# Softmax denominators on VectorE: one reciprocal for each sum, turned and spread, in place of 32 equal ones

## The chip, the cores and the metric

The kernel runs on one core of a Trainium2 chip. The metric is the device time of one execution in microseconds (us): before the change 3507.78 us, the median of three runs (3505.2 to 3508.09).

## The reference

One transformer block with adaptive layer norm, 8 sequences of 1024 tokens of width 512, in float32. Cut to what matters:

```python
mod = silu(condition) @ Wada + bada            # six shifts, gains and gates for each sequence
sh_a, sc_a, gt_a, sh_m, sc_m, gt_m = split(mod, 6)
xm = layernorm(x, g1, be1) * (1 + sc_a) + sh_a
q, k, v = heads(xm @ Wqkv)                     # 16 heads of 32 columns
scores = where(causal, q @ k.T * 32 ** -0.5, -inf)
attn = softmax(scores)                         # exp(s - max) / sum of exp(s - max)
x = x + gt_a * (concat(attn @ v) @ Wproj + bproj)
xm = layernorm(x, g2, be2) * (1 + sc_m) + sh_m
x = x + gt_m * (gelu(xm @ W1 + b1) @ W2 + b2)
```

## The kernel before, in words

The work is cut into 16 blocks of 512 tokens (n, two per sequence). The 16 heads of a block are handled in 4 groups (g) of 4 heads, so there are 64 groups. The keys and queries of a group lie with head and channel on the 128 partitions: head j on partitions 32j to 32j+31.

Attention of a group runs in units. `scores` (L1538) multiplies queries by keys into PSUM (L1595), VectorE adds the causal mask (L1607) and takes row maxima (L1610). The maxima are split into three bfloat16 parts (L1629 to L1632) and turned into rows by TensorE (L1648). `weights_T` (L1663) subtracts the maxima (L1674) and multiplies keys by queries (L1686), ScalarE takes the exponential (L1698), and GpSimd cuts the diagonal (L1703). `weigh` (L1715) multiplies the weights by the values (L1726). `add_weights` (L1801) adds the weights of later keys to those of the first, nearly always on GpSimd (L1816).

`finish` (L1736) ends a group. A matmul with a matrix of ones (L1747) sums the weights over the keys. Its columns are 32 ones for each head, so the sum of head j for token t stands on all 32 partitions of head j: 32 equal rows. ScalarE copies the sums to `rec` (L1756) and the weighted values to `top` (L1759). VectorE inverts `rec` in place in four pieces of 128 columns (`invert`, L1765), and `top` is multiplied by it: by GpSimd in most groups (L1790), by VectorE in three cases. `rec` and `top` have one buffer each, so L1756 of the next group waits for this multiplication. The groups differ in how that is queued:

- the last group of all (`groups[-1]`): inversions and multiplications alternate, piece by piece, at once (L1769 to L1773)
- the last group of block 0 (`first_end`): four inversions and a multiplication on VectorE (L1779), at once
- the other 62: three inversions as jobs, and a fourth job (`quotient`) with the last inversion and the multiplication

The rest of the block is linear work: the projections for k, q, v and the first layer of the MLP by a seven-product scheme (`strassen`), the second layer (`down`) likewise, the output projection (`project_out`), all through `matmul` (L217). Layer norm needs statistics (L619, L620), normalisation (L655, L660), and a turn to channel-first form, for most blocks by VectorE in squares of 32 (L700) and two DMAs (L709, L714). The results of a matmul leave PSUM through `copy_out` (L194, L197) and `combine_out` (L204, L208).

The order of everything is fixed when the program is built. A planner keeps a clock for each engine in `now`; `note` adds a cost in ns to an engine's clock, `due` says when operands are ready. From these clocks `sooner` (L152) picks VectorE or ScalarE, and `either` (L159) picks VectorE (L167) or GpSimd (L170) for an elementwise operation. Jobs wait in one list; `run_jobs` (L558) issues the first job whenever VectorE's clock isn't ahead of TensorE's and its operand is due. `step_aside` (L1457) and `work` (L1423) choose which matmuls come next. So a cost given to `note` decides nothing on the chip itself, but it moves instructions in all queues.

Of the kernel before, what the change touches and what calls it, by code (L numbers as in the profile page):

```python
# [9 lines left out]
F32 = mybir.dt.float32  # L10
# [12 lines left out]
def kernel(  # L23
# [33 lines left out]
    nc = tc.nc  # L57
    B, T, D = x.shape
    HD = W1.shape[1]
    P = 128  # L60
    hd = D // H
    scale = float(hd) ** -0.5
    TB = 512
    NTT = TB // P
    NHALF = T // TB
    NC = D // P
# [15 lines left out]
    small = ctx.enter_context(tc.tile_pool(name="small", bufs=2))  # L82
# [22 lines left out]
    def due(reads=(), writes=()):  # L105
        t = 0.0
        for k in reads:
            t = max(t, written.get(k, 0.0))
        for k in writes:
            t = max(t, left.get(k, 0.0))  # L110
        return t

    def note(engine, ns, reads=(), writes=(), port=False):
        start = max(now[engine], due(reads, writes))
        if port:
            start = max([start] + [b for a, b in pool_spans if a <= start < b])
        end = start + ns
        now[engine] = end
        if engine == "POOL":
            pool_spans.append((start, end))  # L120
            del pool_spans[:-16]
        for k in reads:
            left[k] = max(left.get(k, 0.0), end + SYNC)
        for k in writes:
            written[k] = end + SYNC
        return end
# [9 lines left out]
    def note_pe(ns, form, reads=(), writes=()):  # L136
        now["PE"] = max(now["PE"], due(reads, writes))
        if shape[0] != form:
            shape[0] = form
            now["PE"] += SWITCH  # L140
        note("PE", ns, reads)
        spent[0] += ns
        for k in writes:
            written[k] = now["PE"] + PIPE

    def note_act(ns, func, reads=(), writes=()):
        if func is not None and table[0] != func:
            table[0] = func
            ns += TABLE
        note("ACT", ns, reads, writes)  # L150
# [31 lines left out]
    def lin_bank():  # L182
        i = min(
            (i for i in range(3) if not live[i]),
            key=lambda i: left.get(("l", i), 0.0),
        )
        live[i] = True
        return i
# [54 lines left out]
    def mlp_steps(n):  # L243
        return [("u", n, i) for i in range(NQ)] + [("d", n, part) for part in range(4)]
# [9 lines left out]
    for w in range(1, NB):  # L254
        n = w - 1
        m = mlp_steps(n)
# [29 lines left out]
    n = NB - 1  # L286
# [111 lines left out]
    Q = P // NTT  # L398
# [81 lines left out]
    def spread(o):  # L480
        return cols[:, o : o + NC].unsqueeze(2).to_broadcast([P, NC, B])

    def norm_columns(name, shift_at, gain_at, o_g, o_b):

        gain = const.tile([P, NC, B], F32, tag=f"gain{name}", name=f"gain{name}")
        shift = const.tile([P, NC, B], F32, tag=f"shift{name}", name=f"shift{name}")
        one_plus = small.tile([P, NC, B], F32, tag="onep", name=f"onep{name}")
        nc.vector.tensor_scalar(one_plus, modT[:, ts(gain_at, NC), :], 1.0, None, ALU.add)
        nc.vector.tensor_tensor(gain, one_plus, spread(o_g), ALU.mult)
        nc.vector.tensor_tensor(shift, one_plus, spread(o_b), ALU.mult)  # L490
        nc.vector.tensor_tensor(shift, shift, modT[:, ts(shift_at, NC), :], ALU.add)
        return gain, shift
# [60 lines left out]
    def add_job(job, reads, first=False):  # L553

        at = sum(1 for other in jobs if other[2]) if first else len(jobs)
        jobs.insert(at, (job, reads, first))

    def run_jobs(everything=False):  # L558
        while jobs and (
            everything or (now["DVE"] <= now["PE"] and due(jobs[0][1]) <= now["PE"])  # L560
        ):
            jobs.pop(0)[0]()
# [774 lines left out]
    def perform(step):  # L1337
        kind = step[0]
        if kind == "mod":
            yield from modulation(step[1])  # L1340
        elif kind == "norm_columns_a":
            columns_of["a"] = norm_columns("a", 0, 1, O_G1, O_BE1)
        elif kind == "gates":
            yield from gates(step[1])
        elif kind == "columns_m":
            columns_of["m"] = norm_columns("m", 3, 4, O_G2, O_BE2)
        elif kind == "load_xa":
            x_pre[step[1]] = load_x(step[1])
# [108 lines left out]
    def step_aside(reads, writes):  # L1457


        while threads():  # L1460
            if linear_wait() == NEVER:
                hurry()
            own, other = wait_of((reads, writes)), linear_wait()
            if done_linear[0] < stream["due"]:
                if other > own + 100:
                    break
            elif own <= max(other, 50):
                break
            work()
        while BANK in writes and bank_at() == NEVER:  # L1470
            work()
        run_jobs()
        run_act_jobs()
        run_pool_jobs()
        run_preparation()
# [260 lines left out]
    def finish(n, g):  # L1736

        run_jobs(True)
        acc, slot = totals.pop((n, g))
        more = unadded if (n, g) == first_end else []  # L1740
        step_aside([("acc", n, g), *(("p", slot) for *_, slot in more)], [BANK])
        bank = lin_bank()
        terms = [(0, TB, acc, slot)] + [(c0, w, pT, slot) for parts, pT, slot in more for _, c0, w, _ in parts]
        for i, (c0, w, term, held) in enumerate(terms):
            for j in range(HPG):
                r = slice(j * hd, (j + 1) * hd)
                nc.tensor.matmul(  # L1747
                    banks[bank][r, TB - w :], ones, term[:, j, c0 : c0 + w],
                    start=i == 0, stop=i == len(terms) - 1, skip_group_check=True,
                )  # L1750
            note_pe(2 * COLUMN * w, "columns", [("acc", n, g), ("p", held)], [("l", bank)])
        free_p.extend([slot, *(held for *_, held in more)])
        top = tmp.tile([P, TB], F32, tag="top", name=f"top_{n}_{g}", bufs=1)
        rec = tmp.tile([P, TB], F32, tag="rec", name=f"rec_{n}_{g}", bufs=1)
        kr = "rec"
        nc.scalar.copy(rec, banks[bank])  # L1756
        note_act(585, None, [("l", bank)], [kr])
        live[bank] = False
        nc.scalar.copy(top, outs.pop((n, g)))  # L1759
        note_act(585, None, ["po"], ["top"])  # L1760
        part = TB // 4

        def invert(i):
            some = rec[:, i * part : (i + 1) * part]
            nc.vector.reciprocal(some, some)  # L1765
            note("DVE", 920, [kr], [kr])

        if (n, g) == groups[-1]:
            for i in range(NTT):  # L1769
                invert(i)  # L1770
                some = slice(i * part, (i + 1) * part)
                nc.vector.tensor_tensor(qTs[n][:, g, some], top[:, some], rec[:, some], ALU.mult)
                note("DVE", 200, [kr, "top"], [("att", n, i)])  # L1773
            return

        if (n, g) == first_end:
            for i in range(NTT):
                invert(i)
            nc.vector.tensor_tensor(qTs[n][:, g, :], top, rec, ALU.mult)  # L1779
            note("DVE", 700, [kr, "top"], [("att", n)], port=True)  # L1780
            written["attended", n] = 0.0
            return

        def quotient():
            invert(3)
            if n == NB - 1 and g == NC - 2:
                nc.vector.tensor_tensor(qTs[n][:, g, :], top, rec, ALU.mult)
                note("DVE", 700, [kr, "top"], [("att", n)], port=True)
            else:
                nc.gpsimd.tensor_tensor(qTs[n][:, g, :], top, rec, ALU.mult)  # L1790
                note("POOL", 1285, [kr, "top"], [("att", n)])
            if g == NC - 1:
                written["attended", n] = 0.0

        for i in range(3):
            add_job(lambda i=i: invert(i), [kr], g == NC - 1)
        add_job(quotient, [kr], g == NC - 1)

    shared = {}
# [194 lines left out]
```

## Time and profile before

| | |
|---|---|
| median of three runs | 3507.78 us |
| the profiled execution | 3510.74 us |
| its span, first to last instruction | 3509.0 us |
| TensorE clock granted | 0.998 |
| TensorE (PE) busy | 3454.3 us, 98% |
| VectorE (DVE) busy | 2198.9 us, 63% |
| GpSimd (POOL) busy | 2084.2 us, 59% |
| ScalarE (ACT) busy | 1212.4 us, 35% |

The profile is one execution on the chip. Times are in microseconds unless marked ns; L1765 is line 1765 of the kernel. PE is TensorE's matmul, PEld its weight load, SP the engine that issues most DMAs. A row of a group has the line, engine, operation, destination and sources, shapes and count, then the busy time in us and the mean ns of one, then the idle time of the engine just before and what ended most of it. A row "A <- B: x, y, z" of the waits says that A sat idle for x us in total, y times, longest z, until B was done. A timeline row has start and length in us, engine, line and operation, and in brackets the idle time before it. Matmuls overlap and their ends are modelled, so TensorE's busy time is not all streaming. The "chain" is the work that ended last, followed back from the last instruction.

### The profile page before, as it was taken

How to read it: one execution, taken by the hardware profiler on the slowest of the kernel's cores; microseconds unless marked ns; L12 is line 12 of the kernel's file. 1: busy time of each engine (PE TensorE's matmuls, PEld its weight loads, DVE VectorE, ACT ScalarE, POOL GpSimd, SP SyncE). 2: the span in 40 equal slices, each digit the busy share in tenths (PEclk: the TensorE clock that was granted, in tenths of full speed). 3: DMA queues.
4: the chain of work that ended last, by engine and by line, in shares of the span. 5: the costliest groups of instructions: out<-in, count | busy, mean ns of one | idle time of the engine just before them, and what ended most of it. 6: DMA issues, size and time to landing. Idle time of an engine off the chain costs nothing.

```text
span 3509.0 us, 120365 instructions
## 1 busy us (share of the span) xinstructions
PE 3454.3 (98%) x54429; PEld 1724.0 (49%) x54429; DVE 2198.9 (63%) x2401; ACT 1212.4 (35%) x1276; POOL 2084.2 (59%) x2258
## 2 busy tenths in 40 slices
PE   8999999999999999999999999999999999999999
PEld 4444445445554545445454454544555444554445
DVE  5766676564666656665666566765666756656563
ACT  2335333342233423335223342333423343232531
POOL 3767846666366663756727576275753658537660
PEclk9999999999999999999999999999999999999999
DMA  6843444535545445363454534545354544443334
GB/s 212 263 137 104 137 115 140 142 107 159 142 125 156 119 147 153 119 170 115 137 157 130 155 117 144 150 137 148 116 155 137 165 122 146 128 136 101 96 121 140
DMA packets 328194, 491.10 MB, mean 140 GB/s; under 512 B 27260, under 2 KB 177596, under 8 KB 324100
## 3 DMA queue, kind: packets, MB, share of 16 engines
q1 hardware_dynamic: 327568, 483.39, 47.1%
q8 instruction: 428, 7.01, 0.8%
q14 instruction: 82, 0.67, 0.1%
q10 hardware_dynamic: 116, 0.03, 0.0%
HBM read 425.57 MB, written 55.64 MB: 137 GB/s over the span
## 4 chain that ended last, share of the span: by engine, by line
PE 83%; POOL 7%; DMA 3%; DVE 3%; ACT 1%; issue 1%; SPq 1%; ACTq 0%; DVEq 0%; POOLq 0%
PE bank L217 59%; PE sc L1595 8%; PE st L1686 6%; PE po L1726 6%; POOL pT L1816 4%; PE st L1674 2%; PE bank L1747 2%; DMA hat_m<-held_m 1%; DVE mx L1610 1%; POOL hT L170 1%; ACT pT L1698 1%; DMA held_m<-xm_m 1%; PE bank L1648 0%; POOL xr L170 0%; DMA w<-in_L_cond_Wqkv_dram 0%
## 5 line engine op out<-in xcount | busy, mean ns | idle before, releaser
L1816 POOL TENSOR_TENSOR pT<-pT,pT 128x256 f32<-128x256 f32 (+3 forms) x1254 | 1219.7, 1007 | 298.5 <-PE po L1726 181.6
L1698 ACT ACTIVATE pT<-st 128x2048 f32<-128x2048 f32 x288 | 540.9, 1878 | 1065.1 <-PE st L1686 959.8
L217 PE MATMUL bank<-w,hT 128*32 128x256 f32 x14336 | 823.7, 380 | 0.4 <-issue 0.4
L1610 DVE TENSOR_REDUCE mx<-sc 128x4 f32<-128x2048 f32 (+3 forms) x384 | 665.9, 1755 | 235.6 <-PE sc L1595 229.5
L217 PEld LDWEIGHTS bank<-w,hT 128*32 128x32 f32 x14336 | 446.7, 110 | 390.3 <-issue 105.8
L217 PE MATMUL bank<-xm_m,w 128*32 128x256 f32 x8192 | 498.6, 381 | 3.6 <-ACT xm_m L774 2.2
L217 PE MATMUL bank<-t_m,w 128*32 128x256 f32 x6144 | 382.4, 380 | 0.9 <-DVE t_m L786 0.6
L217 PEld LDWEIGHTS bank<-xm_m,w 128*32 128x32 f32 x8192 | 255.6, 110 | 231.2 <-issue 62.2
L1703 POOL TENSOR_SCALAR_AFFINE_SELECT pT<-pT 128x512 f32<-128x512 f32 x256 | 167.5, 672 | 331.9 <-ACT pT L1698 329.4
L1607 DVE TENSOR_TENSOR sc<-sc,mask 128x1024 f32<-128x1024 f32 (+1 forms) x160 | 162.8, 1018 | 293.3 <-PE sc L1595 237.8
L1595 PE MATMUL sc<-kT,qT 32*128 32x512 f32 (+3 forms) x3072 | 329.5, 521 | 4.3 <-ACT pT L1698 3.3
L1726 PE MATMUL po<-pT,v 128*32 128x512 f32 (+3 forms) x3048 | 301.6, 490 | 3.9 <-POOL pT L1703 3.9
L1686 PE MATMUL st<-qT,kT 32*128 32x512 f32 (+3 forms) x3072 | 300.8, 487 | 0.0
L217 PEld LDWEIGHTS bank<-t_m,w 128*32 128x32 f32 x6144 | 189.6, 110 | 172.9 <-issue 48.5
L1765 DVE RECIPROCAL rec<-rec 128x128 f32<-128x128 f32 x256 | 227.3, 922 | 48.2 <-ACT rec L1756 48.2
L217 PE MATMUL bank<-xm_a,w 128*32 128x256 f32 x3968 | 243.4, 382 | 0.4 <-DMA w<-in_L_cond_Wqkv_dram 0.4
L217 PE MATMUL bank<-w,qT 128*32 128x512 f32 x2048 | 237.0, 595 | 1.1 <-DMA w<-in_L_cond_Wproj_dram 0.7
L1595 PEld LDWEIGHTS sc<-kT,qT 32*128 32x128 f32 x3072 | 129.6, 183 | 188.2 <-issue 88.4
L208 DVE TENSOR_TENSOR hT<-bank,u_u 128x512 f32<-128x512 f32 x187 | 126.6, 686 | 105.8 <-PE bank L217 103.1
L217 PE MATMUL bank<-t_a,w 128*32 128x256 f32 x2944 | 183.2, 380 | 0.0
L217 PEld LDWEIGHTS bank<-xm_a,w 128*32 128x32 f32 x3968 | 123.5, 110 | 110.3 <-issue 29.3
L1115 ACT ACTIVATE hT<-hT,cols 128x512 f32<-128x512 f32 x256 | 164.7, 712 | 35.9 <-DVE hT L208 28.5
(243 smaller groups left out, 3404.0 us busy)
## 6 DMA issues: line engine op xcount, KB each, us to landing
w<-in_L_cond_W_dram SPq DMA_DIRECT2D x384, 256.0 KB
w<-kept_up_S SPq DMA_DIRECT2D x256, 256.0 KB
w<-kept_down_S SPq DMA_DIRECT2D x256, 256.0 KB
w<-kept_qkv_S SPq DMA_DIRECT2D x180, 256.0 KB
w<-in_L_cond_Wqkv_dram SPq DMA_DIRECT2D x147, 256.0 KB
hat_a<-in_x_dram SPq DMA_DIRECT2D x64, 256.0 KB
xr<-in_x_dram SPq DMA_DIRECT2D x32, 512.0 KB
w<-in_L_cond_Wproj_dram SPq DMA_DIRECT2D x64, 256.0 KB
```

The costliest lines, as they stand in the source:

```text
L208: nc.vector.tensor_tensor(out, src, other, op)
L217: nc.tensor.matmul(ps[r, :], columns, rhs, start=start, stop=stop, skip_group_check=True)
L1115: nc.scalar.activation(hT[:, i, :], hT[:, i, :], AF.Gelu, bias=cols[:, O_B1 + f : O_B1 + f + 1])
L1595: nc.tensor.matmul(sc[:, j, c0 : c0 + w], qTs[n][r, gg, ts(qt, P)], keys_of(n, kh)[r, gg, :w], start=True, stop=True, skip_group_check=True,)
L1607: nc.vector.tensor_tensor(place, place, shape_of.to_broadcast(place.shape), ALU.add)
L1610: nc.vector.tensor_reduce(maxima[n, gg][:, kh, qt, :], sc[:, :, c0 : c0 + w], axis=AX.X, op=ALU.max)
L1686: nc.tensor.matmul(st[:, j, c0 : c0 + w], kT[r, gg, ts(k % NTT, P)], qT[r, gg, TB - w :], start=False, stop=True, skip_group_check=True,)
L1698: nc.scalar.activation(pT[:, :, :used], st[:, :, :used], AF.Exp, scale=scale)
L1703: nc.gpsimd.affine_select(diagonal, diagonal, pattern=[[0, HPG], [1, P]], compare_op=ALU.is_ge, fill=0.0, base=0, channel_multiplier=-1,)
L1726: nc.tensor.matmul(po[r, TB - w :], v[:, k % NTT, g * P + j * hd : g * P + (j + 1) * hd], pT[:, j, c0 : c0 + w], start=(k == 0), stop=last ...
L1765: nc.vector.reciprocal(some, some)
L1816: nc.gpsimd.tensor_tensor(into, into, pT[:, j, c0 : c0 + w], ALU.add)
```

## The change

For each group the 128 x 512 tile of sums is handled in squares of 32. `gather(i)` turns 128 columns on VectorE, so that the 32 equal rows of a head become 32 equal columns, and inverts one column of each of the four squares of each head: a reciprocal of 128 x 4 elements in place of 128 x 128. The results go to a new small tile `inverse` (128 x 16). `spread_out` reads each column 32 times over (a stride of zero) and turns it back into `rec`, 512 columns in one instruction, or 128 in the last group. All four gathers are now jobs, and `quotient` has the spreading in place of the fourth inversion. The costs noted change from 920 ns for each of four inversions to 394 ns for each gather (160 + 1.05 x 128 + 100) and 678 ns for the spreading (140 + 1.05 x 512). Two new tiles have one buffer each, and `one_plus`, used in setting up the modulation, has one buffer instead of two.

```diff
-        one_plus = small.tile([P, NC, B], F32, tag="onep", name=f"onep{name}")
+        one_plus = small.tile([P, NC, B], F32, tag="onep", name=f"onep{name}", bufs=1)
...
-        def invert(i):
-            some = rec[:, i * part : (i + 1) * part]
-            nc.vector.reciprocal(some, some)
-            note("DVE", 920, [kr], [kr])
-
+        wide = TB // 4
+
+        def gather(i):
+            squares = small.tile([P, wide], F32, tag="squares", name=f"squares_{n}_{g}_{i}", bufs=1)
+            nc.vector.transpose(squares, rec[:, ts(i, wide)])
+            some = inverse[:, ts(i, wide // Q)]
+            nc.vector.reciprocal(some, squares.rearrange("p (a i) -> p a i", i=Q)[:, :, 0])
+            note("DVE", 160 + 1.05 * wide + 100, [kr], [kr])
+
+        def spread_out(i=0, m=TB):
+            some = inverse[:, i * m // Q : (i + 1) * m // Q].unsqueeze(2).to_broadcast([P, m // Q, Q])
+            nc.vector.transpose(rec[:, ts(i, m)].rearrange("p (a i) -> p a i", i=Q), some)
+            note("DVE", 140 + 1.05 * m, [kr], [kr])
+
+        inverse = small.tile([P, TB // Q], F32, tag="inverse", name=f"inverse_{n}_{g}", bufs=1)
         if (n, g) == groups[-1]:
             for i in range(NTT):
-                invert(i)
+                gather(i)
+                spread_out(i, part)
...
         if (n, g) == first_end:
-            for i in range(NTT):
-                invert(i)
+            for i in range(4):
+                gather(i)
+            spread_out()
...
         def quotient():
-            invert(3)
+            spread_out()
...
-        for i in range(3):
-            add_job(lambda i=i: invert(i), [kr], g == NC - 1)
+        for i in range(4):
+            add_job(lambda i=i: gather(i), [kr], g == NC - 1)
         add_job(quotient, [kr], g == NC - 1)
```

## Prediction, made before the changed kernel was run

> **What bounds the kernel now.** I read the profile's first part, then idle time by stage, then TensorE's waits. The first part has busy time, share of the span, and instructions of each engine:
>
> ```profile
> span 3509.0 us, 120365 instructions
> PE 3454.3 (98%) x54429; PEld 1724.0 (49%) x54429; DVE 2198.9 (63%) x2401; ACT 1212.4 (35%) x1276; POOL 2084.2 (59%) x2258
> ```
>
> TensorE is idle for 3509.0 - 3454.3 = 54.7 us. The change takes work from VectorE, which is idle for 1310 us. It can shorten the run only through TensorE's idle time, or through lateness that its busy time hides. By stage (first number after the stretch: its length, the second: TensorE's busy time):
>
> ```profile
> 0.00:200.00 200.00, 179.25 (x3022) 94.11 (x3026) 137.64 (x175) 52.46 (x62) 103.58 (x134) 1.00 0.71 224
> 200.00:800.00 600.00, 589.64 (x9012) 283.83 (x9004) 381.14 (x403) 234.99 (x233) 398.69 (x433) 0.99 0.43 125
> 3200.00:3509.00 309.00, 299.72 (x4784) 152.41 (x4780) 171.31 (x196) 99.82 (x109) 151.78 (x145) 0.99 0.40 120
> ```
>
> Idle are 20.8, 10.4 and 9.3 us, which leaves 54.7 - 40.5 = 14.2 us for the 2400 us between 800 and 3200. What ended the idle time between 40 and 3380 us, the part where reciprocals run, the longest entries:
>
> ```profile
> PE st L1674 <- DVE mx L1610: 7.8, 8, 2.4
> PE po L1726 <- POOL pT L1703: 3.9, 5, 1.7
> PE bank L1648 <- POOL mcols L1632: 3.3, 4, 1.3
> PE sc L1595 <- ACT pT L1698: 3.3, 6, 0.8
> ...
> PE bank L1747 <- POOL pT L1816: 0.9, 1, 0.9
> ...
> PE bank L217 <- DVE t_m L786: 0.6, 1, 0.6
> ...
> PE sc L1595 <- DVE mx L1610: 0.5, 1, 0.5
> ...
> PE bank L1648 <- DVE hT L208: 0.4, 1, 0.4
> PE bank L217 <- POOL qT L1790: 0.2, 1, 0.2
> ```
>
> No row names the reciprocal (L1765). VectorE ends 7.8 + 0.6 + 0.5 + 0.4 = 9.3 us directly, mostly by row maxima that come late; the splitting of the maxima on GpSimd (L1632), which waits for the same maxima, ends 3.3 us. So 12.6 us, 0.36% of the time, hang on how soon VectorE reaches its work.
>
> **The change, part by part.** These rows price it (a --lines row first, then durations as min/median/max in ns):
>
> ```profile
> L1765 DVE RECIPROCAL rec<-rec 128x128 f32<-128x128 f32 x256 | 227.3, 922 | 48.2 <-ACT rec L1756 48.2
> L1765 DVE RECIPROCAL rec<-rec x256: 887/941/953, 113.5 to 3385.1; 128x128 f32<-128x128 f32 x128
> L636 DVE RECIPROCAL rstd_a<-rstd_a x2: 178/178/179, 11.2 to 51.6; 128x4 f32<-128x4 f32 x2
> L700 DVE STREAM_TRANSPOSE xm_a<-hat_a x56: 653/666/703, 124.3 to 2963.4; 128x512 f32<-128x512 f32 x56
> ```
>
> *Removed:* four reciprocals a group, 4 x 0.941 = 3.76 us.
>
> *Added:* four transposes of 128x128, four reciprocals of 128x4, one transpose of 128x512. The second shape is in the trace: 0.178 us. So is the third: 0.67 us (its source here is a column read with stride zero; no row shows that, and the count of elements written is the same). The first isn't. The two reciprocals give a fixed part: (941 - 178) / 124 = 6.15 ns an element, so 178 - 4 x 6.15 = 153 ns remain at no elements. With the same fixed part a transpose of 128 columns takes 153 + (666 - 153) / 4 = 281 ns. Bounds: 666 / 4 = 167 ns if there were no fixed part, 666 ns if the time didn't depend on size. I take 0.28, between them and from rows of the same engine.
>
> The sum for a group is 4 x (0.28 + 0.178) + 0.67 = 2.50 us, so 1.26 us less than 3.76. With the bounds it is 4 x (0.167 + 0.178) + 0.67 = 2.05 us (1.71 less) or 4 x (0.666 + 0.178) + 0.67 = 4.05 us (0.29 more). For the 62 groups with jobs that is 78 us less work on VectorE (106 less to 18 more), 2% of the span.
>
> [...]
>
> *What lies on the path.* In the 62 job groups, nothing directly: VectorE's queue is what the saving shortens, and TensorE's matmuls cover it. GpSimd's multiplication then sits waiting for the last piece:
>
> ```profile
> L1790 POOL TENSOR_TENSOR qT<-top,rec 128x512 f32<-128x512 f32 x61 | 79.8, 1308 | 123.7 <-DVE rec L1765 123.6
> ```
>
> Those 123.6 us hold GpSimd's queue, but what TensorE gets from there (the diagonals L1703 and the added weights L1816) ended only 3.9 + 0.9 us of its idle time, so I put nothing on it. If the cover went, it would cost what those rows show.
>
> The first block's end runs at once, and there the maximum that TensorE waits for stands right behind the reciprocals:
>
> ```profile
> 171.34 3.39 DVE L1765 RECIPROCAL rec<-rec 128x128 f32<-128x128 f32 x4 [2.00 <-ACT rec L1756]
> 174.84 1.06 DVE L1779 TENSOR_TENSOR qT<-top,rec 128x512 f32<-128x512 f32 x1
> 175.82 2.28 DVE L1610 TENSOR_REDUCE mx<-sc 128x4 f32<-128x2048 f32 x1
> 178.15 1.14 PE L1595 MATMUL sc<-kT,qT 32*128 32x512 f32 x8 [0.51 <-DVE mx L1610]
> ```
>
> The saving of 1.26 us removes this wait of 0.51; next late is nothing of VectorE. The last group's four pieces go from 0.94 to 0.28 + 0.18 + 0.28 = 0.74 us each. They gain nothing: TensorE has work until the projection begins at 3385.79, after the first three pieces are multiplied:
>
> ```profile
> 3377.16 8.82 PE L217 MATMUL bank<-w,hT 128*32 128x256 f32 x160
> 3384.76 0.46 DVE L1772 TENSOR_TENSOR qT<-top,rec 128x128 f32<-128x128 f32 x1
> 3385.79 13.92 PE L217 MATMUL bank<-w,qT 128*32 128x512 f32 x128
> ```
>
> *Beside GpSimd.* Elementwise operations with two sources suffer on VectorE while GpSimd works (L167 goes from 0.69 to 2.87 us, below). Transposes don't, their longest is 703 ns, nor reciprocals, 953 ns, and adds beside them run at their usual length:
>
> ```profile
> 1506.17 2.48 DVE L700 STREAM_TRANSPOSE xm_m<-hat_m 128x512 f32<-128x512 f32 x4
> 1506.33 1.29 POOL L170 TENSOR_TENSOR p_d<-p_d,u_d 128x512 f32<-128x512 f32 x1 [2.67 <-DVE u_d L208]
> 1507.70 1.28 POOL L170 TENSOR_TENSOR p_d<-p_d,row_gm 128x512 f32<-128x512 f32 x1
> ```
>
> *Moved.* The change adds no wait on another engine: gather, reciprocal and spreading follow one another on VectorE, and GpSimd waits for the spreading (0.67) where it waited for the last piece (0.94). No DMA moves by itself, and the single buffer of `one_plus` is used twice in all, on one engine. But the planner's cost per group falls from 3680 to 4 x 394 + 678 = 2254 ns, 1.43 us for 62 groups, or 88 us of its VectorE clock. So jobs come out earlier, and `sooner` and `either` give VectorE some work that ScalarE or GpSimd has now. This reorders all queues, SP's loads too, from the first groups on. The rows can't say in which direction. What they say is how much room there is: the number of switches between score matmuls and column matmuls is set by the units of attention, and TensorE's busy time with them.
>
> *Sum.* The profiled execution took 3510.74 us, 1.74 more than its span and 2.96 more than the median. From it: -0.5 at the first block's end; -2.5 as a third of the 7.8 us of late maxima, a choice, since VectorE has 2% less to do but no reciprocal stands ahead of those eight maxima; 0 elsewhere. That makes 3507.7 for that execution, and on the median's scale 3507.8 - 3 = 3505 us. About 0.2%, 7 us, is what a measurement of this kernel can tell from no change, so this forecast is "same".
>
> **The rivals.**
>
> *Slower: the freed time fills with adds.* `either` compares the two clocks. With 88 us less on VectorE's, adds of L170 become adds of L167, noted at 695 ns but much longer beside a busy GpSimd, and they stand ahead of the maxima. This is in the trace already: before the longest wait for a maximum (the last row is TensorE's).
>
> ```profile
> L167 DVE TENSOR_TENSOR xr<-xr,y_d x15: 691/1312/2867, 364.8 to 3389.9; 128x512 f32<-128x512 f32 x15
> 393.35 1.65 DVE L167 TENSOR_TENSOR t_a<-t_a,xm_a 128x512 f32<-128x512 f32 x1
> 394.93 1.77 DVE L167 TENSOR_TENSOR t_a<-xm_a,t_a 128x512 f32<-128x512 f32 x1
> 396.61 1.22 DVE L1607 TENSOR_TENSOR sc<-sc,mask 128x1024 f32<-128x1024 f32 x1
> 397.87 2.36 DVE L1610 TENSOR_REDUCE mx<-sc 128x4 f32<-128x1024 f32 x2
> 400.28 0.39 PE L1674 MATMUL st<-mrow,minus_ones 32*128 32x512 bf16 x4 [2.42 <-DVE mx L1610]
> ```
>
> If such waits double, they cost another 7.8 + 3.3 = 11 us: 3519 us. It decides from some 7 further waits of the present mean, 7.8 / 8 = 1 us. Against it: adds only move where VectorE's clock is 1.5 us ahead of GpSimd's even with their length, and GpSimd has 41% idle.
>
> *Faster: late VectorE work matters more than the idle time shows.* If shorter queues remove all 12.6 us that hang on VectorE, the time is 3507.8 - 12.6 = 3495 us. For it: weight loads wait for maxima far more often than matmuls do, so lateness lies just under the surface:
>
> ```profile
> PEld L1674 <- DVE mx L1610: 28.7, 50, 2.9
> 3132.66 8.77 PE bank L217 x160
> L217 PE MATMUL bank<-w,hT 128*32 128x256 f32 x14336 | 823.7, 380 | 0.4 <-issue 0.4
> ```
>
> A long stretch takes 8.77 / 160 = 54.8 ns a matmul, this group 823.7 / 14336 = 57.5 on the whole: 5% of its busy time isn't streaming. [...] Against it: the start and end of each stretch are in that 5%, and the change leaves the number of stretches nearly alone.
>
> *It doesn't shorten VectorE's work.* If transposes cost 0.666 whatever their size, VectorE gains 18 us of work that the planner believes gone. With 37% idle on VectorE that gives about 3509 us.
>
> **How the numbers follow.** The forecast (3505, by its own range 3500 to 3512) 0.43; the faster rival 0.30; the slower rival 0.22; no saving 0.05, mostly within 0.2%. So faster by over 0.2%: 0.30; within: 0.47; slower: 0.23. The range reaches past both rivals' times, to 3490 (12.6 us gone and 5 more of the 3.9 + 0.9 + 0.2 us that GpSimd ends) and to 3521 (11 us and 2 for the dearer transposes), with one in ten left out on either side.
>
> **What would show it.** Right: transposes of 128x128 near 0.28 us; VectorE's busy time some 60 to 80 us lower; TensorE's busy time within 5 us of 3454; the wait at the first block's end gone. Wrong: more L167 rows with a larger total in the row of waits for L1610 (slower rival), that row near nothing and GpSimd's wait for `rec` well under 123.6 (faster rival), or a change in TensorE's busy time beyond 5 us, for which the sum has no term.

## The result, and the profile after

The changed kernel takes 3513.13 us (median of 21 runs, 3505.42 to 3516.7), the kernel before in the same series 3508.39 us (21 runs, 3503.79 to 3513.59). The ratio is 1.0013, with a 95% interval of 1.0007 to 1.0019: slower by 0.13%, or 4.7 us between the medians. The forecast was 3505 us, 3 us faster than before. The result is within the 0.2% that the text called "same", but it lies on the other side, its interval doesn't contain 1, and it is outside the forecast's own 3500 to 3512 us, though inside the wide range of 3490 to 3521.

The first part of the profile after, span and busy time of each engine:

```profile
span 3511.4 us, 120687 instructions
PE 3456.8 (98%) x54429; PEld 1723.2 (49%) x54429; DVE 2152.2 (61%) x2744; ACT 1208.0 (34%) x1268; POOL 2083.7 (59%) x2247
```

VectorE has 46.7 us less work than before (2198.9), and TensorE is idle as long as before: 3511.4 - 3456.8 = 54.6 us against 54.7. Its busy time is 2.6 us longer, for the same 54429 matmuls. So the saving on VectorE didn't shorten TensorE's idle time. The new work on VectorE, by groups:

```profile
L1766 DVE STREAM_TRANSPOSE squares<-rec 128x128 f32<-128x128 f32 x256 | 78.6, 307 | 51.1 <-ACT rec L1756 46.1
L1768 DVE RECIPROCAL inverse<-squares 128x4 f32<-128x4 f32 x256 | 45.7, 178 | 8.8
L1773 DVE STREAM_TRANSPOSE rec<-inverse 128x512 f32<-128x512 f32 x63 | 44.7, 709 | 3.2
L1773 DVE STREAM_TRANSPOSE rec<-inverse 128x128 f32<-128x128 f32 x4 | 1.2, 312 | 0.1
```

They add 78.6 + 45.7 + 44.7 + 1.2 = 170.2 us where the reciprocals took 227.3. What ended TensorE's idle time, the entries that answer to those of before, and the new ones (L1565 is a score matmul by single heads, whose maxima are L1582):

```profile
PE st L1674 <- DVE mx L1610: 4.6, 5, 2.8
PE po L1726 <- POOL pT L1703: 4.5, 5, 1.7
...
PE bank L217 <- DMA w<-in_L_cond_Wproj_dram: 3.6, 4, 1.3
PE bank L217 <- ACT u_q L204: 3.5, 1, 3.5
PE sc L1595 <- ACT pT L1698: 3.5, 4, 1.3
...
PE bank L1565 <- DVE mx L1582: 2.3, 1, 2.3
PE bank L1648 <- POOL mcols L1632: 2.3, 3, 1.3
PE sc L1595 <- DVE mx L1610: 1.6, 2, 0.9
```

The waits for maxima were 7.8 + 0.5 = 8.3 us and are 4.6 + 2.3 + 1.6 = 8.5. They moved, and did not shrink. One row is new and stands out: a single wait of 3.5 us for ScalarE's copy of `u_q`. The sums of this pair of profiles don't show a loss by it, since other waits are shorter by as much, and the mean granted clock is 0.998 in both. What the wait is worth has to come from runs.

Comparing the starts of L1756, the copy of a group's sums, shows where time went. After the first block the changed kernel is some 6 us ahead, it is 2.8 us ahead at 1496 us, and 3.2 us behind one group later. In between the lead drifts in steps of up to 3.6 us in both directions (0.3 us are left at 700 us); no other group loses as much as this one. The stretches view over just this group, first the kernel before, then the changed one (length, TensorE's busy time and, behind POOL's, TensorE's clock):

```profile
1496.60:1564.80 68.20, 68.20 (x1081) 34.25 (x1084) 42.84 (x49) 24.23 (x27) 42.03 (x46) 1.00 0.58 168
```

```profile
1493.90:1568.00 74.10, 70.08 (x1088) 34.69 (x1092) 40.70 (x52) 24.78 (x27) 44.87 (x48) 0.98 0.59 171
```

The group takes 5.9 us longer, 4.0 of them idle, and the clock is lower. ScalarE's timeline in the changed kernel, and TensorE's beside it:

```profile
1539.88 0.59 ACT L197 COPY qT<-bank 128x512 f32<-128x512 f32 x1 [0.33 <-PE bank L217]
1545.43 2.93 ACT L774 ACTIVATE xm_m<-hat_m,shiftm,gainm 128x512 f32<-128x512 f32 x4 [4.97 <-DMA hat_m<-held_m]
1548.26 0.56 ACT L204 COPY u_q<-bank 128x512 f32<-128x512 f32 x1
```

```profile
1544.72 0.61 PE L217 MATMUL bank<-t_a,w 128*32 128x256 f32 x8
1548.88 3.21 PE L217 MATMUL bank<-xm_a,w 128*32 128x256 f32 x32 [3.54 <-ACT u_q L204]
```

In the new order four modulations (L774, the scale and shift behind the layer norm) stand in ScalarE's queue ahead of the copy that frees a PSUM bank, and they wait for a DMA, the turn of block 6 to channel-first form. Its first half (L709) goes out 20 us later than in the kernel before; SP's timeline, first of the kernel before, then of the changed one:

```profile
1508.68 0.32 SPq L709 DMA_DIRECT2D held_m<-xm_m  x1
```

```profile
1528.25 0.38 SPq L709 DMA_DIRECT2D held_m<-xm_m  x1
```

TensorE needs the bank and stops. Around the end of the stop, at 1548.88 us, the clock falls to half (the number behind POOL's):

```profile
1545.00:1549.00 4.00, 0.46 (x12) 0.12 (x8) 1.89 (x4) 3.57 (x6) 1.34 (x5) 0.89 0.65 198
1549.00:1551.00 2.00, 2.00 (x20) 0.87 (x24) 0.77 (x2) 0.31 (x1) 1.84 (x2) 0.50 0.02 7
1551.00:1553.00 2.00, 2.00 (x36) 0.97 (x32) 0.69 (x1) 0.00 (x0) 1.92 (x2) 0.87 0.00 0
1553.00:1555.00 2.00, 2.00 (x40) 1.25 (x37) 0.00 (x0) 0.64 (x1) 0.53 (x1) 1.00 0.45 131
```

Behind the stop that costs another 2 x 0.50 + 2 x 0.13 = 1.3 us, which the profile counts as busy time. Together 3.54 + 1.3 = 4.8 us, about the difference of the medians. So far this is an argument from one execution; the experiments test it.

### The profile page after: what moved, and what is told of

It is laid out like the page before. It is cut to its first block, busy times and chain, and to the rows that moved or that the text cites. A ratio compares the mean times of both kernels' runs of the same rounds, so it can differ in the third digit from the quotient of the medians.

```text
span 3511.4 us, 120687 instructions
## 1 busy us (share of the span) xinstructions
PE 3456.8 (98%) x54429; PEld 1723.2 (49%) x54429; DVE 2152.2 (61%) x2744; ACT 1208.0 (34%) x1268; POOL 2083.7 (59%) x2247
## 3 DMA queue, kind: packets, MB, share of 16 engines
q1 hardware_dynamic: 327568, 483.39, 46.7%
## 4 chain that ended last, share of the span: by engine, by line
PE 49%; POOL 4%; DVE 1%; DMA 1%; ACT 1%; issue 1%; SPq 0%; ACTq 0%; DVEq 0%; POOLq 0%
PE bank L217 36%; PE sc L1595 4%; PE st L1686 3%; PE po L1726 3%; POOL pT L1827 3%; PE st L1674 1%; PE bank L1747 1%; POOL hT L170 1%; DMA hat_m<-held_m 0%; ACT pT L1698 0%; DVE mx L1610 0%; DMA held_m<-xm_m 0%; ACT xm_m L774 0%; PE bank L1648 0%; POOL pT L1703 0%
## 5 line engine op out<-in xcount | busy, mean ns | idle before, releaser
L1801 POOL TENSOR_TENSOR qT<-top,rec 128x512 f32<-128x512 f32 x61 | 79.5, 1304 | 200.9 <-DVE rec L1773 181.4
```

## The experiments

Theory A: the operations are covered either way, and the loss comes from the order in which the planner places everything once the noted costs change, through this wait above all. Theory B: the new operations themselves hinder, by their number or beside GpSimd. All ratios are against the kernel before, run on the same chip.

**The new operations in the old order.** The jobs and noted costs are those of before, so that the queues of TensorE, ScalarE, GpSimd and SP are the same, instruction by instruction.

```diff
-            note("DVE", 160 + 1.05 * wide + 100, [kr], [kr])
+            if i < 3:
+                note("DVE", 920, [kr], [kr])
...
-            note("DVE", 140 + 1.05 * m, [kr], [kr])
+            if m == TB or i == 3:
+                note("DVE", 920, [kr], [kr])
...
         def quotient():
+            gather(3)
             spread_out()
...
-        for i in range(4):
+        for i in range(3):
             add_job(lambda i=i: gather(i), [kr], g == NC - 1)
```

> The changed kernel's transposes and small reciprocals, but noted with the old costs (920 ns for each of four pieces) and issued as three jobs and the quotient, so that TensorE, ScalarE and the DMA queue have the order of the kernel before, instruction by instruction. Theory A (the loss is the new order, one wait of 3.5 us of TensorE for ScalarE at 1549 us above all): as the kernel before or up to 6 us faster, 3502 to 3509, and no wait of TensorE over 3 us after the first 20 us. Theory B (the new operations themselves hinder, by their number or beside GpSimd): slower than before by about the 4.7 us of the changed kernel, 3511 to 3515.

Measured: 3510.39 us, ratio 1.0007 (0.9998 to 1.0016). VectorE is busy for 2144.3 us, 54.6 less than before. The interval contains 1; it leaves out a gain of more than 0.7 us, so the 6 us that A allowed for are not there, and it doesn't leave out that the operations hinder a little. There is no wait for `u_q`.

**The old operations in the new order.** The queues of TensorE, ScalarE, GpSimd and SP are those of the changed kernel.

```diff
-            squares = small.tile([P, wide], F32, tag="squares", name=f"squares_{n}_{g}_{i}", bufs=1)
-            nc.vector.transpose(squares, rec[:, ts(i, wide)])
-            some = inverse[:, ts(i, wide // Q)]
-            nc.vector.reciprocal(some, squares.rearrange("p (a i) -> p a i", i=Q)[:, :, 0])
+            some = rec[:, ts(i, wide)]
+            nc.vector.reciprocal(some, some)
             note("DVE", 160 + 1.05 * wide + 100, [kr], [kr])
...
-            nc.vector.transpose(rec[:, ts(i, m)].rearrange("p (a i) -> p a i", i=Q), some)
             note("DVE", 140 + 1.05 * m, [kr], [kr])
```

> The old reciprocals of 128x128 in place, but noted as the changed kernel notes its own (four of 394 ns and 678 ns for a spreading that isn't there), so that TensorE, ScalarE and the DMA queue have the order of the changed kernel. Theory A (order): slower than before by as much as the changed kernel or somewhat more, 3512 to 3518, with the wait of about 3.5 us for ScalarE's copy of u_q. Theory B (operations): as the kernel before, 3506 to 3510.

Measured: 3513.66 us, ratio 1.0014 (1.0005 to 1.0023), as the changed kernel, though the reciprocals are the old ones. The wait is there too, 2.3 us in the profiled execution, which was the slowest of the eleven (3520.7 us):

```profile
PE bank L217 <- ACT u_q L204: 2.3, 1, 2.3
PE bank L217 <- ACT qT L197: 2.1, 1, 2.1
```

The order alone makes the loss; theory B isn't needed for it.

**No inversion at all, in the old order.** This leaves out the inversion, so the weighted values are multiplied by the sums instead of divided by them.

```diff
             some = rec[:, i * part : (i + 1) * part]
-            nc.vector.reciprocal(some, some)
             note("DVE", 920, [kr], [kr])
```

> The order of the kernel before with all 256 reciprocals left out (the weighted values are multiplied by the sums, so part of the computation is missing). It takes 227 us from VectorE and shows the most that any cheaper inversion can give in this order. If TensorE's matmuls cover the inversions, as the prediction says: 3500 to 3508, 0 to 8 us faster. If lateness hidden in TensorE's busy time matters: 3485 to 3497.

Measured: 3507.63 us, ratio 1.0001 (0.9992 to 1.001). VectorE loses over 210 us of work, and TensorE's waits stay:

```profile
PE 3453.9 (99%) x54429; PEld 1722.3 (49%) x54429; DVE 1985.8 (57%) x2145; ACT 1212.5 (35%) x1276; POOL 2087.4 (60%) x2258
```

```profile
PE st L1674 <- DVE mx L1610: 7.2, 7, 2.4
```

The 7.8 us of late maxima are 7.2 with no reciprocal in the kernel. So in this order no cheaper inversion can gain more than the interval allows, 0.08% or 2.8 us, and the third of the late maxima that the forecast took off isn't seen: 0.6 us in place of 2.5.

**The measured costs.** Does the planner misplace work because the changed kernel notes too little?

```diff
-            note("DVE", 160 + 1.05 * wide + 100, [kr], [kr])
+            note("DVE", 485, [kr], [kr])
...
-            note("DVE", 140 + 1.05 * m, [kr], [kr])
+            note("DVE", 180 + 1.04 * m, [kr], [kr])
```

> The changed kernel with the costs that its profile shows (485 ns for a gather, 712 for a spreading) noted in place of 394 and 678; the same operations. If the planner's too low costs are what places work badly (GpSimd's wait for the spread rose from 124 to 181 us): 3503 to 3509. If it is only a chance of the order: anywhere from 3503 to 3516, and the wait of 3.5 us for u_q may stay or go.

Measured: 3512.44 us, ratio 1.0012 (1.0003 to 1.0021). Truer costs don't mend it. The wait for `u_q` is gone, but others have come, 2.8 us for a maximum at 147 us and 2.8 us for an exponential at 1083 us among them.

**The wait removed.** For block 6 alone, the planner is told that the turned rows land later. 8 of 8298 rows of TensorE's order differ from the changed kernel, and 7 of ScalarE's 1268 instructions.

```diff
             note_dma(1250, [("held", key)], [("turned", key)])
+        if key == "m6":
+            written["turned", key] += 6000
         yield [("turned", key)], []
```

> The changed kernel, where the planner is told that the turned rows of block 6 land 6 us later (one extra line for this block). ScalarE then copies the q sums out before the four modulations that wait for that DMA, so the wait of TensorE of 3.5 us at 1549 us should go; 8 of 8298 rows of TensorE's order differ. Theory A (the new order loses through single long waits, each of which can also bring TensorE's clock down to half for 3.4 us, 1.7 us lost): 3.5 to 5.3 us faster than the changed kernel, 3507 to 3510, so back at the kernel before. Rival (the loss is spread over the many small differences of the order): as the changed kernel, 3512 to 3514.

Measured: 3508.09 us, ratio 0.9996 (0.9987 to 1.0005), against 1.0013 (1.0007 to 1.0019) for the changed kernel; the intervals don't meet. The first half of the DMA goes out as late as in the changed kernel (1530.64 us), but three of the four modulations and the work on `u_q` are now on VectorE. On ScalarE the modulation comes with no wait in front of it (lines are two higher in this kernel):

```profile
1549.43 1.88 ACT L1700 ACTIVATE pT<-st 128x2048 f32<-128x2048 f32 x1 [6.58 <-PE st L1688]
1551.21 0.80 ACT L776 ACTIVATE xm_m<-hat_m,shiftm,gainm 128x512 f32<-128x512 f32 x1
1551.91 0.57 ACT L204 COPY qT<-bank 128x512 f32<-128x512 f32 x1
```

Taking this one wait away, with the few moves that go with it, takes the loss away, as theory A has it. But the kernel is then as fast as before, not faster. The profiled execution was the slowest of the eleven (3516.45 us), and not by this stretch: one add of VectorE took 5.79 us, where the changed kernel's took 1.03, and TensorE waited behind it.

```profile
1922.74 5.79 DVE L167 TENSOR_TENSOR xr<-xr,y 128x512 f32<-128x512 f32 x1
1930.79 0.62 PE L1676 MATMUL st<-mrow,minus_ones 32*128 32x512 bf16 x4 [4.25 <-DVE mx L1612]
```

**All inversions done twice, in the old order.** The other side of the cover. (`one_plus` has one buffer here too, as in the change.)

```diff
+            spare = small.tile([P, part], F32, tag="spare", name=f"spare_{n}_{g}_{i}", bufs=1)
+            nc.vector.reciprocal(spare, some)
             nc.vector.reciprocal(some, some)
```

> The order of the kernel before, with every reciprocal of 128x128 done once more into a spare tile: 227 us more for VectorE, 2426 us of 3510. If VectorE's queue is covered by TensorE's work in both directions, as leaving the inversions out suggests (1.0001): within 0.2%, 3505 to 3515. If cover is used up and VectorE's late work shows: over 3518.

Measured: 3558.81 us, ratio 1.0141 (1.0126 to 1.0155), 50 us slower, so the second expectation holds. VectorE is still idle for a third of the time:

```profile
span 3557.0 us, 120597 instructions
PE 3461.9 (97%) x54429; PEld 1728.1 (49%) x54429; DVE 2423.6 (68%) x2657; ACT 1212.4 (34%) x1276; POOL 2086.0 (59%) x2258
```

```profile
PE st L1674 <- DVE mx L1610: 16.4, 20, 2.4
PE sc L1595 <- DVE mx L1610: 7.9, 2, 6.8
```

TensorE's idle time grows from 54.7 to 95.1 us, and the waits for maxima from 8.3 to 24.3; the rest is spread over many other waits. The cover is used up long before the engine is full. A likely reason, not tested, is that the planner has spaced the work for 920 ns and each piece takes twice that.

**Two of four inversions done twice**, with `if i % 2:` in front of the added reciprocal.

> The order of the kernel before, with two of the four inversions of a group done once more into a spare tile: about 114 us more for VectorE. All four doubled cost 50 us, all left out gained nothing. If each doubled inversion hinders by itself: 25 us slower, 3533. If the cover holds up to some load and then breaks: under 10 us slower, 3509 to 3518.

Measured: 3516.32 us, ratio 1.0023 (1.0013 to 1.0034). About 115 us more on VectorE (2314.3) cost 7.7 us, the next 109 cost 42 more. The cover breaks gradually at first, then fast; taking away the 213 us of `no_inversion_old_order` brings nothing that could be measured.

**Only another cost in the kernel before**, 700 and 1000 ns for an inversion, as samples of what a reordering does.

```diff
-            note("DVE", 920, [kr], [kr])
+            note("DVE", 700, [kr], [kr])
```

> The kernel before with nothing changed but the cost that the planner notes for an inversion, 700 ns in place of 920; 461 of 8289 rows of TensorE's order differ. A sample of what a reordering alone does. If the result of the change is the chance of an order: anywhere in 3500 to 3520, and off the kernel before by an amount like the 4.7 us of the changed kernel. If an order made for a shorter inversion is systematically worse: slower by 3 to 8 us.

Measured: 3515.28 us, ratio 1.0017 (1.0008 to 1.0026). The old reciprocals, told to the planner as shorter, lose as much as the change does.

> The kernel before with 1000 ns noted for an inversion in place of 920; 104 of 8289 rows of TensorE's order differ. A second sample of a reordering alone, in the other direction. If chance: anywhere in 3500 to 3520. If lower costs are what hurts, then this one is no slower than before: 3502 to 3509.

Measured: 3510.95 us, ratio 1.0006 (0.9997 to 1.0015): perhaps slower, not settled.

**A second wait removed**, the 2.8 us for a maximum at 394 us in the changed kernel (2.4 before, at 400). The subtractions T3 and T4 of block 3 become jobs behind the maximum, once on top of `wait_removed` (whose profile has it too, 2.77 us) and once in the kernel before.

```diff
-            either(part[out], part[a], part[b], ALU.subtract, [at[a], at[b]], [at[out]])
+            def third(out=out, a=a, b=b):
+                either(part[out], part[a], part[b], ALU.subtract, [at[a], at[b]], [at[out]])
+
+            if key == "a3":
+                add_job(third, [at[a], at[b]])
+            else:
+                third()
```

> The changed kernel with the wait for u_q gone as in wait_removed, and, for block 3 alone, the two subtractions T3 and T4 of its attention input queued as jobs, behind the maxima that TensorE waits 2.8 us for at 394 us. 32 of 8302 rows of TensorE's order differ from wait_removed. Theory A (single long waits decide, at up to 1.7 us of halved clock each beside their own length): 2 to 4 us faster than wait_removed, 3504 to 3507, and so faster than both kernels. Rival (a wait removed comes back elsewhere): 3507 to 3511.

Measured: 3509.3 us, ratio 1.0003 (0.9995 to 1.0012). The wait there is 0.76 us instead of 2.8, the time isn't better than that of `wait_removed`.

> The kernel before with T3 and T4 of block 3 queued as jobs, as in two_waits_removed; 84 rows of TensorE's order differ. Its wait there is 2.4 us. Theory A: 2 to 4 us faster than before, 3504 to 3507. Rival: no change, 3507 to 3511.

Measured: 3507.18 us, ratio 0.9999 (0.9991 to 1.0008). The wait is halved, to 1.2 us, and 1.2 us are less than this interval can show. In `two_waits_removed` theory A's forecast (3504 to 3507) failed: 2 us of a wait were taken away, and their time isn't seen, though the two intervals overlap and could hide part of it. So A holds for the wait for `u_q`, not as a rule that each wait is worth its length. No version beats the kernel before by more than its interval.

## Why the prediction was wrong, point by point

**What bounds the kernel** was right: TensorE's idle time is the same within 0.1 us with 46.7 us less on VectorE, and leaving out every inversion gives 1.0001.

**The price of the operations** was nearly right for the new ones and too high for the old. The transpose of 128x128 took 0.31 us in place of 0.28, the small reciprocal 0.178 as its row said, the spreading 0.71 in place of 0.67, so a group takes 4 x (0.311 + 0.178) + 0.711 = 2.67 us. But four reciprocals in a row don't take 4 x 0.941 = 3.76 us: records of neighbours overlap, and the row of the first block's end in the prediction has 3.39 us for four. Over all 64 groups they kept VectorE busy for 227.3 us, 3.55 us a group. So the saving is 227.3 - 170.2 = 57.1 us, 0.89 us a group, and not 1.26. In the old order VectorE's busy time fell by 54.6 us; in the new one by 46.7, where ScalarE has 8 instructions fewer and GpSimd 11. Both are below the 60 to 80 given.

**The step that failed is "Moved".** The text said that all queues are reordered and that the rows can't say in which direction, and then put nothing on it in the sum. That term measures about +5 us: 1.0014 with the old operations, back to 0.9996 when one stretch of the order is mended. The slower rival named a mechanism that isn't it. Waits for maxima did not double (8.5 us against 8.3), and VectorE did not fill with adds (L167: 221 of them, busy for 260.3 us, against 216 and 260.6); what was late was a DMA in front of ScalarE's copies.

**The 2.5 us off the late maxima** were wrong: they stay at 7.2 us with no inversions. The text itself said that no reciprocal stands ahead of those maxima, and should have drawn the conclusion.

**The 0.5 us at the end of the first block** were wrong: the score matmul waits 0.89 us where it waited 0.51. The step from the first inversion to the multiplication is 167.29 - 164.17 = 3.12 us where it was 174.84 - 171.34 = 3.50, so 0.4 us shorter and not 1.26. The multiplication behind it took 1.46 us in place of 1.06, which takes that back, and TensorE has 0.4 us less other work in front of the matmul in the new order:

```profile
164.17 0.31 DVE L1766 STREAM_TRANSPOSE squares<-rec 128x128 f32<-128x128 f32 x1 [2.02 <-ACT rec L1756]
...
166.47 0.71 DVE L1773 STREAM_TRANSPOSE rec<-inverse 128x512 f32<-128x512 f32 x1
167.29 1.46 DVE L1790 TENSOR_TENSOR qT<-top,rec 128x512 f32<-128x512 f32 x1
168.67 2.28 DVE L1610 TENSOR_REDUCE mx<-sc 128x4 f32<-128x2048 f32 x1
171.00 1.14 PE L1595 MATMUL sc<-kT,qT 32*128 32x512 f32 x8 [0.89 <-DVE mx L1610]
```

**The faster rival** fell: GpSimd's wait for `rec` rose from 123.6 to 181.4 us, and TensorE's waits for maxima are as long in sum as before. "It doesn't shorten VectorE's work" fell too.

**What stays open.** Whether the new operations alone hinder: by up to 0.16% in the old order (1.0007, 0.9998 to 1.0016), while `wait_removed`, which has them too, is at most 0.05% above the kernel before. Whether an order planned for a shorter inversion is worse as a rule: all three with lower costs (394 and 678, measured costs, 700) are slower clear of noise, the one with a higher cost is not settled, and four orders are too few to tell a rule from chance. Why the new order issues the DMAs of block 6 some 20 us later was not traced to a single decision of the planner. Why one add took 5.79 us in one execution. And why the second wait's time didn't come back.

## What to carry to other kernels

Before pricing a cheaper operation, leave it out in the old order: here that run says at once that no way of inverting can gain more than 2.8 us. Where the order is planned from noted costs, a new cost is a change of its own, and the four orders made in this way (394 and 678, measured costs, 700, 1000) have medians 2 to 6 us above the one before, the last within its interval; the two parts can be told apart by the new operations with the old costs, and the old operations with the new. Idle time of an engine isn't slack to fill either: VectorE, idle for 37%, cost 50 us when 225 us were added in places that the plan had spaced for less.

## What the runs showed of the hardware

In one run a wait of TensorE of 2.42 us was followed by a granted clock of half for 3.4 us, so that the wait and this stretch together cost 1.7 times the wait; in another run a wait of the same length was followed by a clock of 1.00. Before the score rows at 400.28 us in the kernel before, TensorE waits 2.42 us, and the clock stays at 1.00 (the stretches begin at the end of the wait; TensorE's clock stands behind POOL):

```profile
400.28:402.28 2.00, 1.98 (x40) 0.96 (x44) 1.91 (x3) 1.17 (x2) 1.77 (x5) 1.00 0.00 0
402.28:404.28 2.00, 2.00 (x44) 0.80 (x36) 0.00 (x0) 1.77 (x2) 1.30 (x2) 1.00 0.23 81
```

With the new operations in the old order the same wait, again 2.42 us, is followed by this:

```profile
397.49 0.40 PE L1674 MATMUL st<-mrow,minus_ones 32*128 32x512 bf16 x4 [2.42 <-DVE mx L1610]
```

```profile
397.49:399.49 2.00, 2.00 (x16) 0.61 (x20) 1.90 (x3) 0.79 (x2) 1.77 (x5) 0.68 0.00 0
399.49:401.49 2.00, 2.00 (x32) 0.99 (x28) 0.00 (x0) 2.00 (x2) 0.90 (x2) 0.50 0.24 87
401.49:403.49 2.00, 2.00 (x36) 0.91 (x28) 0.00 (x0) 0.15 (x1) 1.92 (x3) 0.97 0.78 226
```

The loss is 2 x (0.32 + 0.50 + 0.03) = 1.7 us, which is 3.4 us at half the clock, and it appears as busy time. The stretch at 1549 us in the changed kernel is as long: (4 x 0.11 + 2 x 0.50 + 2 x 0.13) / 0.50 = 3.4 us, and it began before the wait was over. So a clock of half was there around the waits of 2.42 us and 3.54 us in these two executions and not behind the wait of 2.42 us in a third; what decides between them was not shown. Whether it comes may be part of the 10 us by which executions of one kernel differ (3503.79 to 3513.59 us for the kernel before), and so may a single long instruction like the add of 5.79 us; that was not tried.
